# Quantised feed-forward rows: copied into float32r tiles by DMA and transposed in that type, thirteen batches of sixteen

## The chip, the cores and the metric

The kernel runs on one core of one Trainium2 chip. The metric is the device time of that core in microseconds. Before the change the median of 3 runs is 645.22 us (645.11 to 645.31).

## The reference

The input `x` has 16 batches of 256 rows and 256 columns. One layer is computed:

```python
x = x + attn(cond(x))                   # cond: 16-head attention, RMS norm, shift and gain from `cond_256`
                                        # attn: a time mix with a decaying scan, three projections, one out
x = x + ffn(rotate(x))                  # rotate: a quaternion rotation of the columns
# ffn: every matmul has both operands rounded to FP4 in blocks of 16 and scaled back
h = silu(xq @ w_gate.T) * (xq @ w_up.T) # 256 -> 704
y = fp4(h) @ fp4(w_down).T              # 704 -> 256
```

The rounding `fp4` takes the largest magnitude of each block of 16, divides it by 6 to get a scale, rounds each element to the grid 0, 0.5, 1, 1.5, 2, 3, 4, 6, and multiplies the scale back. The change concerns the rows of `fp4(h)`.

## The kernel before

**Stages.** Each batch passes a chain of generators: `ask` (load, query, key and value projections), `attend` (scores, exponentials, weighted values), `leave` (output projection, norm), `mix` (time mix), `rotate`, `hidden` twice, `turn_h` twice, `down`. `hidden(b, tt)` handles 128 of the 256 rows: for each of two column ranges (0 to 384, 384 to 704) PE makes the gate and the up product (L1003), ACT takes a tanh (L1015), DVE forms h in PSUM (L1017, L1019) and `quant_bank` rounds it: DVE instructions on L554 to L557, an absolute value on ACT (L559), two more on DVE (L561, L562), and a product on POOL (L564) that writes the rounded range into an SBUF tile `hq` of 128 x 704 float32, of which there are four buffers.

**Transposing.** `turn_h(b, tt)` makes two calls of `turn_part` (L604 to L609), each of three PE transposes of 128 columns (the last of six has 64) from `hq` into a PSUM bank; ACT copies them into `hT` (L1033 to L1037). The first call reads only the first column range, the second only the second. `down` then multiplies `hT` by `downT` (L1072 and L1079, or L1052 for the late batches). The same `turn_part` serves `out_weights` for the down weights. The last three batches (`late`) use another layout in `rotate` and `down`.

**The order of the work.** There is no scheduler at build time. `ORDER` is a list of 1884 steps written out: `h4` means "run the generator of `hidden(4, 0)` to its next yield". The instructions of PE, ACT, DVE, POOL and SP (SyncE, which issues nearly all DMAs) stand on each engine in just that order, and each engine works through its own list in order, waiting on semaphores. `BANKS` gives, one digit per use, the PSUM bank that each intermediate takes. The letters are a `ask`, t `attend`, l `leave`, m `mix`, r `rotate`, h and i `hidden` for the two row tiles, d and e `turn_h` for them, f `down`; the digit after it is the batch in hexadecimal.

**SyncE's queue.** It issues the input rows (`load_x`, L165), for each spread of queries or keys a store of the split tile to a scratch tensor `kept` in device memory (L704) and eight loads back from it (L708) that wait for the store to land, and the output rows (L1091, or L1064 for late batches).

**float32r.** From batch 2 on the attention scores (L771) take float32r operands: `spread` DMAs float32 bits into a tile declared float32r with a `bitcast`. The plain matmuls and all transposes are float32.

Of the kernel before, what the change touches and what calls it, by code (L numbers as in the profile page):

```python
# [8 lines left out]
F32 = mybir.dt.float32  # L9
BF16 = mybir.dt.bfloat16  # L10
F32R = mybir.dt.float32r
# [7 lines left out]
P = 128  # L19
# [6 lines left out]


ORDER = """
L af L Q L W1 a0 Q L Q a0 Q V0 a0 a1 a0 a0 a1 L W1 a0 W5 Q V0 L Q W1 a1 a1 a1 t0 a1 t0 K t0 W1 K W4 a0 t1 L W5 L
t1 a2 L t1 a2 W5 K W1 t0 W4 K W0 W4 K t0 R V0 a2 a3 M K A a3 a0 t0 L a1 W4 W5 a1 a2 M t0 K A t1 R t1 L t0 t0 t1  # L30
t0 W2 R O t0 t1 t0 W5 M T O W2 t1 t0 t0 a2 t1 V0 t0 a4 t1 L t1 t1 t0 t1 W3 t0 M t0 a2 W4 t1 W1 a2 t1 R V0 A l0
a2 R l0 a2 M W0 l0 V0 W0 W3 l0 W5 M A t1 W3 A t1 l0 W2 t1 T a3 R l0 l0 a2 m0 l0 a3 l1 A l1 W0 m0 m0 R W1 m0 m0
m0 m0 m0 a2 l1 a2 m0 l1 t2 W5 V0 R t2 t2 t2 a3 m0 V1 m0 m0 t2 t2 m0 W3 l1 t2 W3 m0 l1 m0 t2 t2 t2 t2 R t2 t2 t2
R m0 V0 t2 W0 W0 l1 m1 a3 W4 a3 a3 m0 V0 W3 l1 t2 m1 W3 a3 t2 t2 W2 W2 W0 A m1 m1 l2 A m1 m1 W4 l2 r0 m1 l2 m1
l2 r0 a4 a3 m1 m1 l2 l2 m1 m1 l2 m2 m1 m1 l2 m1 a3 m2 t3 a3 t3 m2 t3 t3 t3 m1 a4 t3 r0 r0 t3 r0 t3 a4 t3 t3 t3
m2 a4 t3 t3 a5 m2 W2 a4 V1 m2 t3 a4 t3 r0 t3 m2 m1 r0 t3 r0 a4 r1 m2 m2 a4 r1 t3 r1 r0 a4 W2 a5 a4 l3 l3 a6 m2
l3 V1 r1 m2 r0 a5 i0 a5 m2 i0 r1 r1 m2 i0 l3 V1 a4 t4 r1 m2 t4 t4 h0 i0 V1 t4 t4 i0 V1 m2 a5 t4 i0 h0 i0 h0 h0
t4 t4 i0 V1 t4 t4 t4 t4 i0 t4 a5 l3 t4 a5 r1 l3 r1 t4 m2 m2 h0 l3 a5 m3 l3 m3 t4 V1 a5 m3 i0 i0 a5 r2 r1 t4 h0
t4 m3 m3 r2 i0 m3 h0 a5 m3 l4 l4 a6 m3 l4 m3 m3 i0 a6 a5 l4 m3 m3 V1 a6 m3 t5 m3 t5 i1 i0 m3 t5 t5 i0 m3 t5 t5
e0 h0 i1 i1 e0 a6 t5 i1 t5 t5 t5 t5 h0 t5 t5 m3 i1 l4 t5 r2 a6 r2 t5 r2 l4 a7 t5 l4 i1 i1 d0 h0 i1 a6 h0 m4 r3  # L40
l4 m4 m4 h0 a6 a6 t5 d0 h1 m4 h0 r3 r2 i1 t5 h1 h1 a6 a6 i1 h1 m4 m4 h0 a7 r2 h1 i0 i1 h0 a6 h1 m4 a7 m4 a7 i1
m4 t6 h1 e0 t6 m4 m4 e0 t6 m4 l5 t6 i1 l5 t6 t6 r2 h0 d0 l5 m4 i1 h1 i1 t6 r2 m4 a7 m4 t6 d0 t6 l5 l5 t6 t6 r3
t6 t6 r3 t6 l5 a7 r2 e1 l5 r3 m4 a7 t6 d1 r3 i2 a7 r3 a7 f0 i1 i2 h2 i2 r3 i2 r3 f0 m5 l5 h2 e1 m4 a7 m5 a8 i2
h2 m5 h2 a7 i2 i2 h2 h1 r4 h2 h1 a7 h2 h1 d1 f0 h1 t7 i2 f0 t6 t7 f0 r4 t7 t7 h1 e1 t7 h1 m5 t7 t6 e1 t7 m5 h1
a8 t6 t7 m5 t7 t7 t7 a8 r4 h1 m5 t7 h2 d1 a8 r4 t7 d1 m5 r4 a8 a8 d2 l6 t7 m5 l6 l6 l6 i2 m5 i2 i2 r4 r3 m5 a8
i2 m5 r4 a8 l6 m5 h2 t7 a8 m5 h2 i2 h2 a8 m5 f1 l6 i2 m5 i2 i3 a9 a8 h2 h2 l6 i3 f0 f1 i3 h2 f1 i3 a8 l6 h2 m6
h2 d2 m6 m6 t8 f1 t8 t8 t7 t8 e2 i2 f1 i3 m5 t8 d2 r5 i3 i3 d2 r5 t7 a9 t7 t8 t8 t8 e2 t8 i3 e2 t8 a9 t8 a9 t8
t8 e3 m6 l7 m6 t8 l7 m6 t8 a9 r4 h3 h3 l7 l7 a9 r4 m6 m6 a9 l7 h3 e2 m6 a9 h3 l7 h3 a9 m6 m6 h3 f2 l7 i3 a9 i3
m6 i3 m6 h3 f2 i3 l7 m7 h3 m6 i3 i3 m6 m6 a9 aa m7 h3 i3 h3 h3 f1 h3 f2 m7 a9 e3 t9 t8 t9 t9 t9 f2 m6 r4 d3 f2
i3 t9 r6 h3 h3 t9 d3 e3 t8 h3 r6 t8 t9 h3 aa t9 t9 d3 e3 r5 r5 t9 r5 aa i4 i4 t9 l8 d3 t9 i4 m7 i4 aa i4 ab r5  # L50
h4 l8 i4 r5 m7 l8 h4 i4 f2 l8 aa t9 h4 h4 aa t9 m7 r5 h4 h4 l8 l8 i4 m7 h4 l8 t9 m7 m7 aa aa h4 m7 m7 i4 m7 m7
d4 m8 i4 i4 f3 aa aa l8 m7 m8 h4 m7 i4 i4 f3 m7 h4 m7 i4 m8 aa d4 r7 f3 h4 aa h4 i4 h4 ta f3 ta ta t9 f3 ta r7
ab h4 ac h4 ta e4 r7 t9 ab r7 e4 ta ab i4 ta r7 h4 r5 t9 ta ta r7 m8 ta ta ta ta r7 d4 r5 r6 ab r6 ta m8 m8 e4
m8 ab ab ta r6 m8 m8 m8 m8 l9 ab r6 h5 l9 m8 i5 h5 r6 i5 d4 m8 ab h5 l9 i5 h5 ab i5 e4 h5 i5 h5 h5 h5 ab l9 i5
m8 m8 r6 h5 h5 h5 tb h5 tb ta tb i5 tb m8 m8 r6 ab h5 l9 f4 tb l9 tb tb h5 i5 h5 tb e5 f4 ta ta e5 tb h5 tb tb
tb l9 f4 d5 r8 f4 f4 l9 tb r8 d5 r6 d5 ac m9 f4 tb r7 r8 r7 la tb la h6 h6 la r8 r8 h6 i5 i5 h6 m9 la d5 h6 la
i5 r7 i5 m9 m9 la ac m9 r8 m9 i5 m9 m9 ac i5 m9 la m9 ma m9 ac i6 m9 i7 m9 ac r8 h6 r8 ac m9 i5 i5 m9 i6 i6 ac
e5 m9 ac i7 h6 ac la i7 h6 ma e5 i6 f5 i7 f5 i6 i7 ma i6 i7 m9 f5 ad i6 f5 d6 h7 r9 h6 i6 i7 h6 h6 h6 ac f5 h7
h7 ac d6 tc tc r9 h6 tb h6 h7 tc ad tc ad ae h7 tc tc h6 tb h7 tc ad h7 tc tc tb r9 tc ad tc tc i7 ma h7 tc r9
h6 d6 ad i6 r9 ma tc e6 ma ad tc i6 i6 ma i6 h7 r9 r9 i7 f5 ma i6 r8 ma ad e6 r8 i6 lb ad h7 i7 h7 i6 h8 ma i6  # L60
i7 ma ad i7 ma e6 ma h7 h8 d6 i7 lb ad r9 e6 i7 h8 ma h7 ma r9 lb h7 i7 h8 td lb tc h7 ad td h8 td td td ma h8
lb h8 td e7 lb lb f6 lb f6 e7 mb td f6 i7 mb tc mb h8 ma tc h7 td td d7 f6 ra d7 i8 td f6 td i8 td ra r9 td e7
ae i8 i8 td d7 ra i8 mb i8 e7 f6 ra i8 i9 ae d7 i9 mb ra mb i9 i9 lc ra mb ae mb td h8 mb lc ae h8 i9 lc i8 i9
lc ra ae i9 lc mb h8 ae lc h8 mb h9 lc ra h8 mc ae h8 h9 h9 ra ae mb h9 ae h8 mb mb td d8 lc i8 h9 i8 mb h9 mc
mb f7 ra f7 h8 i8 mb i8 h9 f7 td d8 mc f7 te i8 f7 te rb rb ae te te td e8 i8 rb te te mc h9 i8 mc mc ae rb e8
af f3 rb ld ld rb i9 mc mc mc te ld rb mc te ld te mc mc te te ld mc te i8 te mc mc te mc te d8 af te e8 ld af
te e9 ld md h9 i9 h9 ld h9 te md md md af i9 af d8 mc af i9 md h9 md C rb i9 rb h9 af ha af md i9 e8 i9 md md h9
ha ha md ha f8 md ia ia ha af ia md md ia ha af h9 ia f8 md md i9 f8 ia ia af tf e9 rb tf f8 rc tf tf ia d9 tf
f8 ha tf ia md tf rc tf d9 tf rc i9 ha ia ia tf ia tf tf rc tf tf ia ea e9 e9 ib da rc tf h9 tf d9 ib ib f7 ia
ia le rc rc ib tf f8 le hb ib d9 hb rc tf hb ib le ha le hb le ha ib f9 rc le f9 md le hb ha hb da me ia ha le  # L70
hb ib ha f9 f9 ha ea ha rc ea me ea f9 eb me me me rd ha ib da hb ib me ib me db rd ib rd me rd lf me ib hb da
lf hb ib lf rd rd lf hb lf ib me rd me rd hb lf me hb me lf lf me rd rd ib fa fa hb me db mf eb hb eb hb fa me
db mf mf hc ic hc hc db me fa hc mf re ic fa ic hc ic re hc hc eb re mf ic re ic mf hc re re mf f9 fb re dc hc
fb hc re ic hc dc mf hc mf mf hc re mf mf hc ic ec hc fb mf ic ec ic hc hd ic mf dc mf re id ic ie mf hd ic dc
mf id fb id ic ic id ic hd rf hd id ec ec fc fb id ie rf rf ie id id fb rf fc hd rf ed id hd ed id id hd fc id
hd rf hd rf dd hd id rf ie dd hd he rf id hd he rf id id hd he ed hd he if ie ed hd hd ie if ie ie ie ie ie ie
dd dd he if if ie he he he fa fd ee he fd fd de ee if he ie he if he hf ie fd ie hf he if de he hf if ee he if
ee if ef if hf he hf de de hf fe if fe hf hf hf if hf hf if hf df hf if if fe ef hf hf C fc fe ff df ef ef hf fd
df df C fc fe C ff fc ff ff ff ff ff
"""  # L80


BANKS = """
0123456702 1345670521 3470521364 7320516473 0275164237 5164023571 6043175415 3752406175 2406137541 6035741604
3165042763 1504276315 0246701245 6012465307 2164375023 4756234571 0254371254 3172130671 2507136254 7163204617
3246172530 2615304527 0615627045 6207341502 6731502617 0341635042 3570143527 6013756021 3750425405 6130253607
4163075165 3210746251 0736251063 2416521425 7045273645 0273165407 3416523071 4530276135 2074630146 5370462715
3064537106 2536713460 2153470134 6702346753 6154321675 3421673245 7054763473 1052674273 1520731207 3561403256
1743256412 3054167401 5274301574 3065120373 4561207356 3074305126 4732065704 3215431275 0312670435 1274531604
7531045261 0675105402 5137205146 7250136247 5013473506 2435264053 7415602417 2516427460 3561207314 5017264210  # L90
7640327125 3020425264 6026516106 4106452410 156014205
"""


@with_exitstack
def kernel(
    ctx: ExitStack,
    tc: tile.TileContext,
    x: bass.AP,
    cond: bass.AP,  # L100
    mask: bass.AP,
    w_q: bass.AP,
# [22 lines left out]
    nc = tc.nc  # L125
# [29 lines left out]
    def ps():  # L155
        return bank("ps")
# [41 lines left out]
    early = const.tile([P, T2], F32, tag="early", name="early")  # L198
    nc.scalar.activation(early, mhalf, AF.Exp)
    ident = const.tile([P, P], F32, tag="ident", name="ident")  # L200
    make_identity(nc, ident)


    blank = const.tile([P, P], F32, tag="blank", name="blank")
# [398 lines left out]

    def turn_part(src, k0):  # L604
        pt = ps()
        for k in range(k0, k0 + 3):
            n = min(P, FF - k * P)
            nc.tensor.transpose(pt[0:n, (k - k0) * P : (k - k0 + 1) * P], src[:, k * P : k * P + n], ident)  # L608
        return pt[:, 0 : 3 * P].rearrange("p (k t) -> p k t", t=P)  # L609

    def out_weights(t):
# [407 lines left out]
            nc.vector.scalar_tensor_tensor(h[:, 0:n], th, 0.5, h[:, 0:n], ALU.mult, ALU.mult)  # L1019
            if f0 == 0:  # L1020
                hq = wk.tile([P, FF], F32, tag="hq", name="hq", bufs=4)
                hqs[b, tt] = hq
            yield from quant_bank(h, n, hq[:, f0 : f0 + n])


    def turn_h(b, tt):
        hq = hqs.pop((b, tt))
# [234 lines left out]
```

## Time and profile before

| | |
|---|---|
| median of runs | 645.22 us |
| profiled execution | 645.53 us |
| its span | 643.7 us |
| PE busy | 635.6 us (99%), 3936 matmuls |
| DVE busy | 579.0 us (90%) |
| ACT busy | 391.2 us (61%) |
| POOL busy | 161.4 us (25%) |
| L608, PE transposes of `hq` | 204, durations 272 to 331 ns |
| L564, POOL's product into `hq` | 64, 0.79 us mean |
| DMA traffic | 57.72 MB, 29.4% of 16 engines on SyncE's queue |
| granted PE clock | 1.00 |

The profile is of one execution. A PE instruction's duration runs from its start to a modelled end and overlaps the next; the time from one start to the next is what it costs in a full stream. A plain float32 matmul stands as two records (a weight load and a matmul, twice), a transpose or a float32r matmul as one. In a group's line stand the number of instructions, their busy time, the mean duration of one in ns, and the engine's idle time ahead of them with what ended it. In a line of the timeline stand the start in us, the duration of the merged stretch, and the group.

### The profile page before, as it was taken

To read this page: it belongs to the slowest core of one execution; us is meant where nothing else is said; L and a number is where in the kernel's file an instruction comes from. 1 tells how busy PE (TensorE), PEld (TensorE's weight loads), DVE (VectorE), ACT (ScalarE), POOL (GpSimd) and SP (SyncE) were. 2 spreads that over 40 slices of the span, in tenths; PEclk is the share of its full clock that TensorE was granted. 3 is DMA by queue.
4 is the path that set the end of the run, shared out by engine and by line. 5 is a ranking of instruction groups with operands and counts; after the bars stand their busy time and mean duration, and the time that the engine had idled before them with its cause. 6 is when DMAs were issued, how large, how long until landed. Compare 5 with 4: busy or idle time off the path is not lost.

```text
span 643.7 us, 11304 instructions
## 1 busy us (share of the span) xinstructions
PE 635.6 (99%) x3936; PEld 475.9 (74%) x3936; DVE 579.0 (90%) x1178; ACT 391.2 (61%) x903; POOL 161.4 (25%) x214
## 2 busy tenths in 40 slices
PE   9999999999999999999999999999999999999996
PEld 7568877677777778777777777777877778776675
DVE  7897899889898877999998999999999999999994
ACT  3879784776757577674766546666483755433332
POOL 3353213222231122131221313113130122112220
PEclk9999999999999999999999999999999999999999
DMA  6643525334251425333420334203204100001001
GB/s 169 172 149 120 167 87 174 99 99 133 82 166 35 154 57 166 78 100 116 148 67 18 126 102 149 67 17 131 82 34 151 47 2 16 1 1 35 0 26 46
DMA packets 62848, 57.72 MB, mean 90 GB/s; under 512 B 36912, under 2 KB 40896, under 8 KB 62784
## 3 DMA queue, kind: packets, MB, share of 16 engines
q1 hardware_dynamic: 62416, 56.65, 29.4%
q8 instruction: 33, 0.54, 0.4%
q10 hardware_dynamic: 368, 0.28, 0.1%
q14 instruction: 31, 0.25, 0.1%
HBM read 38.03 MB, written 18.87 MB: 88 GB/s over the span
## 4 chain that ended last, share of the span: by engine, by line
PE 83%; DVE 12%; issue 2%; ACT 1%; DVEq 0%; ACTq 0%
PE ps L632 24%; PE ps L1003 18%; PE ps L793 9%; PE ps L644 8%; PE ps L1072 7%; PE pss L771 5%; PE ps L608 3%; PE ps L965 2%; PE pss L763 2%; DVE v L562 1%; DVE ps L554 1%; PE ps L656 1%; DVE ps L561 1%; DVE ps L1019 1%; PE ps L1079 1%
## 5 line engine op out<-in xcount | busy, mean ns | idle before, releaser
L1003 PE MATMUL ps<-guT,xqT 128*128 128x320 f32 (+1 forms) x512 | 165.6, 461 | 0.6 <-DVE v L562 0.6
L781 ACT ACTIVATE w<-pss 128x512 f32<-128x512 f32 x256 | 133.6, 609 | 32.7 <-PE pss L771 28.8
L1003 PEld LDWEIGHTS ps<-guT,xqT 128*128 128x128 f32 x512 | 94.7, 190 | 42.0 <-DVE v L562 1.7
L564 POOL TENSOR_TENSOR hq<-v,am 128x320 f32<-128x320 f32 (+1 forms) x64 | 50.0, 787 | 175.8 <-DVE v L562 154.4
L698 POOL TENSOR_TENSOR two<-two 128x512 f32<-128x512 f32 x28 | 35.7, 1275 | 114.2 <-ACT two L691 79.1
L793 PE MATMUL ps<-w,v_one 128*32 128x256 f32 x1024 | 63.1, 382 | 0.1
L559 ACT ACTIVATE m<-ps 128x384 bf16<-128x384 f32 (+1 forms) x64 | 29.8, 467 | 53.2 <-DVE ps L557 52.9
L1072 PE MATMUL ps<-hT,downT 128*128 128x256 f32 x260 | 59.6, 379 | 0.0
L1072 PEld LDWEIGHTS ps<-hT,downT 128*128 128x128 f32 x260 | 48.8, 190 | 8.1 <-ACT w L781 0.3
L936 DVE RECIPROCAL den<-den 128x512 f32<-128x512 f32 x16 | 53.5, 3343 | 0.1
L793 PEld LDWEIGHTS ps<-w,v_one 128*32 128x32 f32 x1024 | 31.8, 109 | 25.3 <-ACT w L781 3.6
L1015 ACT ACTIVATE th<-ps 128x320 f32<-128x320 f32 (+1 forms) x64 | 29.8, 469 | 26.9 <-PE ps L1003 26.1
L771 PEld LDWEIGHTS pss<-qT,kT 64*128 64x128 f32 x448 | 31.0, 185 | 19.3 <-issue 8.9
L771 PE MATMUL pss<-qT,kT 64*128 64x256 f32 x448 | 42.6, 306 | 0.1
L561 DVE SCALAR_TENSOR_TENSOR ps<-m,ps 128x384 f32<-128x384 bf16 (+1 forms) x64 | 33.2, 518 | 6.0 <-ACT m L559 5.8
L562 DVE SCALAR_TENSOR_TENSOR v<-m,ps 128x384 f32<-128x384 bf16 (+1 forms) x64 | 33.3, 521 | 4.9
L557 DVE SCALAR_TENSOR_TENSOR ps<-ps,rs 128x320 f32<-128x320 f32 (+1 forms) x64 | 34.1, 533 | 2.2
L554 DVE TENSOR_REDUCE ps<-ps 128x20 f32<-128x320 f32 (+1 forms) x64 | 34.1, 532 | 2.2
L608 PE MATMUL ps<-ident,hq 128*128 128x128 f32 (+1 forms) x204 | 34.5, 283 | 0.4 <-POOL hq L564 0.2
L1019 DVE SCALAR_TENSOR_TENSOR ps<-th,ps 128x320 f32<-128x320 f32 (+1 forms) x64 | 33.2, 518 | 1.1 <-PE ps L1003 0.4
L1017 DVE SCALAR_TENSOR_TENSOR th<-th,ps 128x320 f32<-128x320 f32 (+1 forms) x64 | 32.1, 507 | 0.4 <-ACT th L1015 0.3
L608 PEld LDWEIGHTS ps<-ident,hq 128*128 128x128 f32 (+1 forms) x204 | 22.0, 136 | 13.1 <-issue 4.0
(200 smaller groups left out, 1288.2 us busy)
## 6 DMA issues: line engine op xcount, KB each, us to landing
kept<-two SPq DMA_DIRECT2D x28, 512.0 KB, 3.2
qT<-kept SPq DMA_DIRECT2D x112, 128.0 KB, 2.9
kT<-kept SPq DMA_DIRECT2D x112, 128.0 KB, 2.8
x_sb<-in_x_dram SPq DMA_DIRECT2D x64, 64.0 KB, 2.3
out_dram<-o_sb SPq DMA_DIRECT2D x52, 64.0 KB, 1.9
out_dram<-o_sb SPq DMA_DIRECT2D x6, 128.0 KB, 2.3
raw<-in_L_ffn_w_down_dram SPq DMA_DIRECT2D x2, 352.0 KB, 3.9
raw<-in_L_ffn_w_gate_dram SPq DMA_DIRECT2D x5, 128.0 KB, 3.3
```

The source lines that it names most:

```text
L554: nc.vector.tensor_reduce(top, blk(x), AX.X, ALU.max, apply_absolute_value=True)
L562: nc.vector.scalar_tensor_tensor(v, m, BASE, x, ALU.max, ALU.subtract)
L564: nc.gpsimd.tensor_tensor(blk(dst), blk(v), bc(am), ALU.mult)
L608: nc.tensor.transpose(pt[0:n, (k - k0) * P : (k - k0 + 1) * P], src[:, k * P : k * P + n], ident)
L632: nc.tensor.matmul(pool_tile[:, ot * n : (ot + 1) * n], w[:, ct, ot * P : (ot + 1) * P], src[ct], start=(ct == 0), stop=(ct == E2 - 1),)
L644: nc.tensor.matmul(pool_tile[:, tt * E : (tt + 1) * E], srcT[:, ct, tt * P : (tt + 1) * P], w[:, ct, :], start=(ct == 0), stop=(ct == E2 - 1),
L771: nc.tensor.matmul(quad[2 * s + r][:, i * S : (i + 1) * S], kT[rows_, 2 * r + i, g, ks], qT[rows_, 2 * r + i, g, :], start=True, stop=True,)
L781: nc.scalar.activation(w[kt][:, r].rearrange("p i q -> p (i q)"), quad[r], AF.Exp)
L793: nc.tensor.matmul(pu[32 * r : 32 * r + 32, i * S : (i + 1) * S], vo[:, kt, 8 * g + 2 * r + i, :], w[kt][:, r, i, :], start=(kt == 0), sto ...
L936: nc.vector.reciprocal(flat(den), flat(den))
L1003: nc.tensor.matmul(p_[:, 0:n], xqT[:, ct, tt * P : (tt + 1) * P], guT[:, ct, base : base + n], start=(ct == 0), stop=(ct == E2 - 1),)
L1072: nc.tensor.matmul(pdn[:, 0:S], downT[:, k, h * P : (h + 1) * P], hT[:, k, :], start=(k == 0), stop=False)
```

## The change

For the thirteen batches that are not late, `hidden` issues a DMA on SyncE's queue after each of its two column ranges, from `hq` into a new tile `hr` of type float32r with two buffers. `turn_h` gets `hr` instead of `hq`. `turn_part` sees the type and transposes with an identity of type float32r, `ident_r`, made once by an ACT copy, into a float32r view of the PSUM bank. The bits are moved as they are. `hidden` has two steps more per row tile, 52 in all, so `ORDER` has 1936 steps; it and `BANKS` are written anew throughout. The work of the stages is otherwise the same.

```diff
+    ident_r = const.tile([P, P], F32R, tag="ident_r", name="ident_r")
+    nc.scalar.copy(ident_r, ident)
...
     def turn_part(src, k0):
         pt = ps()
+        fast_ = src.dtype == F32R
         for k in range(k0, k0 + 3):
             n = min(P, FF - k * P)
-            nc.tensor.transpose(pt[0:n, (k - k0) * P : (k - k0 + 1) * P], src[:, k * P : k * P + n], ident)
+            dst = pt[0:n, (k - k0) * P : (k - k0 + 1) * P]
+            nc.tensor.transpose(
+                dst.bitcast(F32R) if fast_ else dst, src[:, k * P : k * P + n], ident_r if fast_ else ident
+            )
...
             if f0 == 0:
                 hq = wk.tile([P, FF], F32, tag="hq", name="hq", bufs=4)
-                hqs[b, tt] = hq
+                if not late(b):
+                    hr = wk.tile([P, FF], F32R, tag="hr", name="hr", bufs=2)
+                hqs[b, tt] = hq if late(b) else hr
             yield from quant_bank(h, n, hq[:, f0 : f0 + n])
-
+            if not late(b):
+                nc.sync.dma_start(out=hr[:, f0 : f0 + n].bitcast(F32), in_=hq[:, f0 : f0 + n])
+                yield
```

A stretch of `ORDER` from the same part of the pipeline, before and after (the whole list is different in this way):

```diff
-m2 a4 t3 t3 a5 m2 W2 a4 V1 m2 t3 a4 t3 r0 t3 m2 m1 r0 t3 r0 a4 r1 m2 m2 a4 r1 t3 r1 r0 a4 W2 a5 a4 l3 l3 a6 m2
+a4 t3 m2 a4 t3 m1 r0 V1 t3 r0 t3 t3 m2 a4 r1 t3 a4 m2 r0 t3 t3 r0 a4 V1 V1 r0 r1 a4 m2 a4 r0 m2 i0 r1 t3 a5 i0
```

## The prediction

> **What bounds the kernel now.** I read the page's first two parts, then the busy time of each engine in stretches of 40 us, the groups of PE instructions with shapes kept apart, PE's timeline around 312 us, and the waits on SyncE's queue. The first part and the slices:
>
> ```profile
> PE 635.6 (99%) x3936; PEld 475.9 (74%) x3936; DVE 579.0 (90%) x1178; ACT 391.2 (61%) x903; POOL 161.4 (25%) x214
> ...
> PE   9999999999999999999999999999999999999996
> ...
> DVE  7897899889898877999998999999999999999994
> ```
>
> PE has no free slice. Its ends are modelled, so I checked starts: over the whole span PE's matmuls begin only some 9.5 us later in sum than their own cadence would let them, 2.5 us of that in the first 6 us and 3.4 us after 560 us. PE really is full. But look at DVE after the first third:
>
> ```profile
> 280.00:320.00 40.00, 39.96 (x257) 31.05 (x256) 36.94 (x74) 25.03 (x51) 10.63 (x11) 1.00 0.40 125
> ...
> 400.00:440.00 40.00, 40.00 (x247) 30.20 (x246) 38.01 (x79) 26.28 (x67) 8.80 (x12) 1.00 0.20 62
> 480.00:520.00 40.00, 40.00 (x242) 29.36 (x241) 38.38 (x81) 20.12 (x47) 7.42 (x8) 1.00 0.31 93
> ```
>
> (Columns: stretch, PE, PE weight loads, DVE, ACT, POOL busy, granted clock, DMA share, GB/s.) DVE is busy 38.0 to 38.4 of 40 us from 360 to 600 us, and the rest are its gaps of a few tens of ns between instructions, 1.3 to 1.9 us per stretch. Its real idle time, 31 us over the span, lies nearly all before 360 us. So in the first half PE alone sets the pace, in the second PE and DVE both. A microsecond taken from PE is worth a microsecond only if the order lets DVE start its work that much earlier.
>
> **The change, part by part.**
>
> *The transposes.* Of 204 transposes on L608, 156 (13 batches, 2 row tiles, 6 each) change to float32r.
>
> ```profile
> 313.21 0.55 PE L608 MATMUL ps<-ident,hq 128*128 128x128 f32 x3
> 313.59 1.03 PE L965 MATMUL ps<-x1T,rotP 128*128 128x256 f32 x4
> 314.46 0.49 PE L608 MATMUL ps<-ident,hq 128*128 128x128 f32 x3
> 314.79 1.89 PE L632 MATMUL ps<-xT,wt_k 128*128 128x256 f32 x8
> ```
>
> Three take 0.33 us from start to next start (314.46 to 314.79), 109 ns each; a group behind a tiled matmul shows 0.38. The price in float32r is not in the trace. Bounds: 109 ns (no gain) and 54 ns (half). The nearest row is the attention score, the only float32r matmul here:
>
> ```profile
> L771 PE MATMUL pss<-qT,kT 64*128 64x256 f32 x448 | 42.6, 306 | 0.1
> L608 PE MATMUL ps<-ident,hq 128*128 128x128 f32 x170 | 31.1, 285 | 0.4 <-POOL hq L564 0.2
> ```
>
> Scores run in pairs on two halves of the rows, and inside a group of eight a pair starts every 118 ns: 256 columns in 118 ns, and two weight loads of 128 columns in the same 118. An f32 matmul of 256 columns takes 216 ns per record, and two records each (L632 shows 128 records for 64 calls). So one float32r pass moves a column in about half the time that an f32 record does, and one float32r weight load costs about 59 ns when it overlaps a matmul. A transpose has one load and 128 columns: I take 60 ns, saving 49.
>
> Two rules of the Trainium skill speak against that. "TensorE: Matmul & The Clock Gate", Back-to-back issue gap, says that a stream of load and matmul pairs at 128 columns sustains one per about 81 ns, not the 56 of an isolated matmul. Then the saving is 28 x 156 = 4.4 us instead of 49 x 156 = 7.7. The same page, Part 4: PE-mode transpose, puts a transpose in a kernel at about 275 ns, most of it access latency, which a type could not change. The trace has both: durations of 272 to 331 ns, but starts 109 ns apart, so the latency is overlapped and the cadence counts. I stay with 60, as the load cadence of 59 is this chip's row, and keep 81 and 109 for the range. PE's sum: -7.7 us (-4.4, 0).
>
> *The copies.* 52 new copies on SyncE's queue, hq to hr, 192 or 160 KB, 9.4 MB beside today's 57.7. Near rows: out rows of 128 KB land in 2.3 us, raw weights of 128 KB in 2.4 to 3.3, a 512 KB store in 3.2; issue takes about 0.45 us. I take 3 us from issue to landing (2 to 5 in a crowd). A half row now needs, after DVE's last quantising instruction (L562), POOL's product (0.79 us), the issue and the landing: about 4.2 us instead of 1. Does the order leave room? Counting the work of PE or of DVE (the larger) that stands in the order between that DVE instruction and the first transpose that reads its half: the old order leaves 1.3 us at the least, the new one at least 5.3 us for all 52 halves. So copies are hidden with 1 us over at the tightest, at no cost to PE; if that cover fails, each late one costs what it is late, and behind the transpose in PE's queue stands everything else. The three late batches keep the short path.
>
> *SyncE's queue.* A copy waits for POOL, and also for the transposes of the row tile two before (hr has two buffers). What stands behind it: attention's stores and loads, x loads, output stores.
>
> ```profile
> SPq L704 <- POOL two L698: 118.5, 21, 22.9
> SPq L1091 <- DVE o_sb L1086: 100.5, 4, 52.0
> SPq L708 <- DMA kept<-two: 73.2, 28, 4.3
> ```
>
> The queue already spends most of its time waiting for others, 52 x 0.45 = 23 us of issue fit in it. The other way: a spread holds the queue for its store's landing (73.2/28 = 2.6 us) and eight loads of 0.59 us, 7.3 us together, and 13 of the 52 copies stand directly behind such loads. I cost this at 0 when the order is kept, and at the third rival when not.
>
> *Small things.* One ACT copy of ident at the start, under ACT's 14 us of idle there: nothing. DVE, ACT and POOL do the same work as before; evictions of hT are unchanged. hq comes free at the copy's landing, not at the transpose.
>
> *The order.* PE's list now has the same instructions in another sequence, so I compared where PE hands over to DVE. Summing PE's start-to-start times up to a place in the order and DVE's work behind that place (durations times 0.93, since they overlap: 650 us of them fill 605 us of busy time and gaps), the largest such sum is about what the time cannot fall below. Before: 531.5 + 110.9 = 642.4 us, against a span of 643.7, so this floor is tight. After, each changed transpose 49 ns cheaper: 523.5 + 113.4 = 636.9. The floor falls by 5.5 us, not 7.7: the rest goes to DVE, which in the new order gets busy earlier (up to 300 us PE and DVE advance side by side) but still ends as the bound. If transposes stay at 109 ns the same sum is 641.2.
>
> The sum: profiled execution 645.5 us (span 643.7), minus 5.5 = 640.0; the median of the runs is 645.2, 0.3 less, so 639.7. I give nothing extra for stalls or for better packing: **639.7 us**.
>
> **The rivals.**
>
> *A, forecast:* PE is relieved and DVE lets 4.4 x 0.7 to 7.7 us of it through: 637 to 642.5. For: no added work on a full engine, and room of 5.3 us before every changed transpose. Against: second half of the span is DVE's too.
>
> *B, the change does not do what it says:* float32r transposes are bound by the weight load, or by both reads together, and stay at 109 ns. Order alone gives 641.2 - 642.4 = -1.2, and some wait for a copy gives +1 to +2: 644 to 646.5. For: a transpose loads new weights each time, and L608's loads are 140 ns long. Against: those loads start 109 ns apart while overlapping matmuls, and the scores' loads at 59.
>
> *C, slower:* copies land after PE wants them, because SyncE's queue serves in order. Place: ten of the 52 copies have less than 8 us in the order between DVE's last instruction and the transpose (5.3 to 7.3). A copy that comes behind a spread waits on average half of its hold, 3.6 us, and in the crowd may land in 5 us instead of 3, so 4.2 us becomes up to 9.8 and the ten miss by 2.5 to 4.5 us. The gain of 5.5 us is cancelled from a mean miss of 0.55 us over the ten; at 1.5 us each, on an engine with no free slice, it is 15 - 5.5: 655, and about 650 where every third falls on a PE that DVE holds up anyway. For: the queue's waits reach 23 and 52 us, and each tile's copy also waits for hr. Against: seven of the ten stand behind 500 us, where attention's traffic has ended (the DMA digits are 0 to 4), and the middle copy has 18 us.
>
> *D:* the second half is DVE's so fully that PE's relief turns into PE idle time: 643.5 to 645.
>
> **How the numbers follow.** A 0.62, B 0.08, C 0.25, D 0.05. A difference of 0.2% (1.3 us) is about what a measurement of this kernel tells from none. A is faster; half of D and a quarter of B are faster; within 0.2% are the other half of D and most of B; C is slower, save a small part that ends level. Faster 0.66, same 0.08, slower 0.26. A's own range is 636 to 642.5. For 8 in 10 I reach below to 635 (all 7.7 us and 2 of waits gone) and above into C to 650.
>
> **What the profile of after would show.** Transposes of hr in threes at about 0.18 us from start to next start (0.24 by the skill's 81 ns, 0.33 if B). PE's busy sum smaller by 5 to 8 us with DVE at 91%. Copies hr from hq landing in 2 to 4 us. In PE's and its loader's waits, hr named by a DMA for less than 2 us in sum; 5 us or more is C. DVE's waits before 360 us smaller by some 5 us; if they stay at 31 us, it is D. What would make the forecast wrong altogether: an order whose waits come from somewhere that neither PE's nor DVE's sums show, such as ACT's evictions of hT standing behind exponentials.

## The result and the profile after

The changed kernel takes 652.07 us, the median of 4 runs (651.33 to 654.54), beside 645.26 (645.11 to 645.35) for the kernel before in the same session: a ratio of 1.0113, with a 95% interval of 1.0086 to 1.0139. It is slower, where faster was forecast, and 2 us above the range. One run of the kernel e9 below (670.68 us, at a granted clock of 0.947) fell in a slower state of the core and is left out of its figures. The profiled execution took 652.05 us with a span of 650.3, 6.5 more than the 643.7 before.

The first two parts of the page of the kernel after:

```profile
PE 633.0 (97%) x3936; PEld 472.6 (73%) x3936; DVE 580.3 (89%) x1178; ACT 393.4 (61%) x904; POOL 161.9 (25%) x214
...
PE   8999999999999999999999999999999999997996
DVE  6988998798998998889998999999899899999993
PEclk9999999999999999999999999999999999999999
```

PE's busy sum fell by 2.6 us only, and PE is no longer full: the slices at the start and at about 595 us show it. The granted clock is full up to 647 us, behind PE's last matmul, so in this execution no part of the loss is a slower array. The same in stretches of 40 us (columns as in the prediction), first before, then after:

```profile
440.00:480.00 40.00, 39.87 (x277) 29.98 (x277) 38.15 (x72) 24.70 (x55) 9.47 (x12) 1.00 0.24 73
560.00:600.00 40.00, 39.62 (x178) 28.73 (x177) 38.06 (x80) 13.35 (x32) 8.20 (x9) 1.00 0.06 14
```

```profile
440.00:480.00 40.00, 38.74 (x217) 29.86 (x216) 36.97 (x72) 25.33 (x61) 9.68 (x13) 1.00 0.34 104
480.00:520.00 40.00, 38.98 (x252) 28.45 (x254) 36.52 (x73) 22.52 (x55) 6.92 (x7) 1.00 0.35 109
560.00:600.00 40.00, 36.62 (x162) 26.48 (x161) 37.91 (x80) 13.30 (x35) 6.57 (x8) 1.00 0.11 32
```

Behind 440 us PE loses 1.1, 1.0 and 3.0 us against before, and DVE, which the forecast wanted busier, loses 1.2 and 1.9 in the first two of them. PE's waits over the span of after, longest first (us in sum, times, longest):

```profile
PE ps L614 <- DMA hr<-hq: 2.3, 2, 1.9
PE pss L779 <- DVE res L1097: 1.3, 1, 1.3
PE ps L614 <- ACT m L563: 1.2, 1, 1.2
PE ps L599 <- DVE num L934: 1.1, 1, 1.1
```

Before, the longest of PE's waits was 1.0 us. The first line names two late copies. The 1.2 and 1.3 us name ACT and DVE; the experiments below show that a DMA stands behind both.

Six transposes before, then six after, each with the matmul behind it, from PE's timeline (start, duration of the merged stretch). Both groups stand behind eight attention scores:

```profile
231.39 0.88 PE L608 MATMUL ps<-ident,hq 128*128 128x128 f32 x6
232.10 1.89 PE L632 MATMUL ps<-yT,wt_ao 128*128 128x256 f32 x8
```

```profile
305.08 0.74 PE L779 MATMUL pss<-qT,kT 64*128 64x256 f32 x8
305.75 0.70 PE L614 MATMUL ps<-ident_r,hr 128*128 128x128 f32 x6
306.29 1.10 PE L973 MATMUL ps<-x1T,rotP 128*128 128x256 f32 x4
```

Six take 0.71 us to the next start before. After, they take 0.54, but the matmul behind them is then held. Counted over all groups, the weight loads inside a group start 84 to 85 ns apart (109 before), and the first full float32 matmul behind the group runs 280 ns to its successor instead of 216. A group of three between full float32 matmuls of 256 columns costs 250 ns instead of 330, so 27 ns each; taken over all 52 groups with their neighbours it is 3.2 us, 21 ns for each of 156.

The copies themselves (KB each, median us from issue to landing):

```profile
hr<-hq SPq DMA_DIRECT2D x26, 192.0 KB, 2.4
hr<-hq SPq DMA_DIRECT2D x26, 160.0 KB, 2.1
```

The trace tells the landing of seven of the 52: six took 2.1 to 2.8 us and one 4.2.

The end of the span is 6.5 us later: PE's last matmul starts 5.3 us later (643.8 for 638.5) and what follows it takes 1.2 us more.

### The profile page after: what moved, and what is told of

Same layout as the page of the kernel before. It is cut to its first block, busy times and chain, and to the rows that moved or that the text cites. A ratio compares the mean times of both kernels' runs of the same rounds, so it can differ in the third digit from the quotient of the medians.

```text
span 650.3 us, 11454 instructions
## 1 busy us (share of the span) xinstructions
PE 633.0 (97%) x3936; PEld 472.6 (73%) x3936; DVE 580.3 (89%) x1178; ACT 393.4 (61%) x904; POOL 161.9 (25%) x214
## 4 chain that ended last, share of the span: by engine, by line
PE 67%; DVE 22%; issue 3%; ACT 3%; DMA 2%; SPq 2%; POOL 0%; DVEq 0%; ACTq 0%; POOLq 0%
PE ps L640 20%; PE ps L1011 14%; PE ps L801 9%; PE ps L652 7%; PE pss L779 5%; PE ps L1084 4%; PE ps L614 2%; DVE v L566 2%; PE ps L973 2%; DVE ps L558 2%; DVE ps L1027 2%; DVE ps L561 2%; DVE ps L565 1%; DVE th L1025 1%; DVE rs L560 1%
## 5 line engine op out<-in xcount | busy, mean ns | idle before, releaser
L563 ACT ACTIVATE m<-ps 128x320 bf16<-128x320 f32 (+1 forms) x64 | 29.7, 464 | 44.3 <-DVE ps L561 44.0
L566 DVE SCALAR_TENSOR_TENSOR v<-m,ps 128x320 f32<-128x320 bf16 (+1 forms) x64 | 33.3, 521 | 4.7
L1025 DVE SCALAR_TENSOR_TENSOR th<-th,ps 128x320 f32<-128x320 f32 (+1 forms) x64 | 32.1, 506 | 4.3 <-ACT th L1023 4.1
L947 POOL TENSOR_TENSOR yT<-num,den 128x512 f32<-128x512 f32 x16 | 20.5, 1278 | 58.4 <-DVE den L944 50.9
L565 DVE SCALAR_TENSOR_TENSOR ps<-m,ps 128x320 f32<-128x320 bf16 (+1 forms) x64 | 33.1, 518 | 1.1 <-ACT m L563 0.9
L652 PE MATMUL ps<-wt_v,xT 128*128 128x256 f32 x128 | 30.7, 382 | 0.0
```

Of the source, the lines that this page charges most:

```text
L566: nc.vector.scalar_tensor_tensor(v, m, BASE, x, ALU.max, ALU.subtract)
L652: nc.tensor.matmul(pool_tile[:, tt * E : (tt + 1) * E], srcT[:, ct, tt * P : (tt + 1) * P], w[:, ct, :], start=(ct == 0), stop=(ct == E2 - 1),
```

## The experiments

Three things changed at once: the order with its banks, the type of the transposes, the copies. The first four runs take them apart. Theory after the result: the order and late copies both cost more than the transposes give. Rivals: the order alone; the copies alone; the float32r transposes bring nothing. Diffs of `ORDER` and `BANKS` are given in words.

**e1, the order alone.** The new `ORDER` with its `BANKS`, no copies, float32 transposes. `hq` gets six buffers instead of four and two of `hr`; the yields stay, so that the steps count as in after.

```diff
-                hq = wk.tile([P, FF], F32, tag="hq", name="hq", bufs=4)
-                if not late(b):
-                    hr = wk.tile([P, FF], F32R, tag="hr", name="hr", bufs=2)
-                hqs[b, tt] = hq if late(b) else hr
+                hq = wk.tile([P, FF], F32, tag="hq", name="hq", bufs=6)
+                hqs[b, tt] = hq
...
             if not late(b):
-                nc.sync.dma_start(out=hr[:, f0 : f0 + n].bitcast(F32), in_=hq[:, f0 : f0 + n])
                 yield
```

> The new order with neither copies nor float32r: rows stay in hq (6 buffers, the room that hr had), 156 transposes in plain float32. If the new order itself loses the time (theory 1: its start and its last 60 us leave PE waiting whatever the type), this stays at 652 or goes up by the 3 us that float32 transposes cost more: 652 to 656. If late copies lose it (theory 2), taking them away gives back about 5 us of waits and pays 3 us for the type: 648 to 650. If neither, and only the small gain of the type was mis-sized, it is near the old kernel: 645 to 647.

Measured: 652.63 us, 1.0099 (1.0082 to 1.0116). The order alone costs 6.4 us, nearly the whole loss of after. Its span is 7.1 us longer than before. PE's late starts (beyond the time to the next start that the same pair of instructions usually shows) sum to 16.1 us instead of 11.5: 3.0 more in the first 80 us, 2.7 more between 560 and 600, 1.1 less elsewhere. (By the profile's own idle gaps of 150 ns and more it is 7.7 us instead of 2.5.) What follows PE's last start grew by 1.7, and 0.8 lies in the cadence of the other sequence and was not placed. The stretch around 595 us of e1, in windows and on the timeline (in brackets the idle time ahead and what ended it):

```profile
560.00:600.00 40.00, 37.16 (x162) 26.68 (x161) 37.77 (x79) 13.19 (x35) 6.31 (x7) 1.00 0.06 14
```

```profile
593.59 1.34 PE L1011 MATMUL ps<-guT,xqT 128*128 128x320 f32 x4 [0.89 <-DVE v L566]
595.15 0.52 PE L614 MATMUL ps<-ident,hq 128*128 128x128 f32 x3 [0.21 <-DVE th L1025]
596.59 0.52 PE L614 MATMUL ps<-ident,hq 128*128 128x128 f32 x3 [0.93 <-issue]
597.67 2.64 PE L1081 MATMUL ps<-hT,downT 128*128 128x256 f32 x11 [0.56 <-DVE th L1025]
```

PE stands four times in 4 us: the two `hidden` row tiles, their transposes and `down` follow each other in PE's list. What they wait for is a PSUM bank (one of the eight that take PE's products), not data. The lines name L566 and L1025, on which DVE reads the bank of h, or of the gate product, for the last time. Walking `ORDER` and `BANKS` with the trace's times bears this out: each of the four begins 0.05 to 0.15 us after the last reader of its bank has ended (the third one's is an ACT copy on L978), while the two transposes' rows were written 0.7 and 1.2 us before; and when each wait began, none of the eight banks was free, so no other digit would have helped there. Over the whole span 4.1 of e1's 7.7 us of idle time end this way, beside 0.8 of 2.5 us before. No copy and no float32r is in this kernel.

**e2, copies without the type.** After, with `hr` declared float32.

```diff
-                    hr = wk.tile([P, FF], F32R, tag="hr", name="hr", bufs=2)
+                    hr = wk.tile([P, FF], F32, tag="hr", name="hr", bufs=2)
```

> The new order with the 52 copies, but hr is plain float32 and all transposes are float32: the type alone undone. The profile of the changed kernel shows a group of three at about 250 ns in place of 330 between full matmuls, about 330 in place of 386 behind tiled ones: 3 us over 52 groups. Type worth its 3 us: 654 to 656. Type worth the 7.7 us that was forecast: 659. Type worth nothing, because PE waits elsewhere anyway: 651 to 653.

Measured: 657.61 us, 1.0157 (1.0119 to 1.0196), with a wide spread (653.36 to 658.86). Against e1 the copies cost 0.58%, 3.7 us. In the profiled execution (658.86 us) most of this is the clock. PE waits 1.74 us for keys up to 507 us and 1.90 us for a copy up to 603 us, and behind each wait the granted clock is 0.50 for 3.41 us:

```profile
504.85:508.26 3.41, 1.67 (x14) 1.21 (x15) 3.34 (x8) 0.89 (x3) 1.64 (x2) 1.00 0.45 150
508.26:511.67 3.41, 3.41 (x11) 2.31 (x10) 1.52 (x4) 1.76 (x5) 0.00 (x0) 0.50 0.00 0
600.42:603.83 3.41, 1.51 (x10) 1.23 (x11) 3.20 (x9) 1.88 (x5) 0.18 (x1) 1.00 0.42 112
603.83:607.25 3.42, 3.42 (x10) 2.70 (x9) 3.17 (x8) 0.92 (x3) 0.84 (x1) 0.50 0.09 20
```

At half the clock 3.41 us are 1.7 us of PE's work lost, 3.4 us for both. e1's trace has no such stretch before its end.

**e3, the type without copies, in the new order.** As e1, but POOL writes its product into a float32r tile. POOL then rounds the value to float32r, where the copy moves the bits; nothing else is left out here or in the later kernels of this kind.

```diff
+                hq = wk.tile([P, FF], F32 if late(b) else F32R, tag="hq", name="hq", bufs=6)
```

> The new order, float32r transposes, no copies: POOL's product writes the row as float32r at once, which rounds the quantised values (that part of the computation is changed). Against the changed kernel only the copies are gone. Theory 2 (late copies): 645 to 648. Theory 1 (order): 650 to 652.

Measured: 648.69 us, 1.0051 (1.0032 to 1.0071). Against e1 the type brings 0.48%, 3.1 us; after, which has the copies too, is 0.62% or 4.0 us slower than e3. So the sum is 6.4 for the order, minus 3.1 for the type, plus 4.0 for the copies: 7.3 us, where 1.13% of 645.26 is 7.3. (The intervals of e3 and after don't touch; each term is uncertain by about 1 to 2 us, and the sum closes by its making.)

PE's list in e3 is the same as in after, so each late copy can be found by laying one against the other. From 20 to 330 us there is no difference. Then there are three places: at 335 us PE starts 1.25 us later, at 459 us 1.7, at 500 us 0.3. The first two on the timeline of after:

```profile
336.22 0.42 PE L614 MATMUL ps<-ident_r,hr 128*128 128x128 f32 x3 [1.23 <-ACT m L563]
...
461.80 0.71 PE L779 MATMUL pss<-qT,kT 64*128 64x256 f32 x7 [1.26 <-DVE res L1097]
...
597.51 0.40 PE L614 MATMUL ps<-ident_r,hr 128*128 128x128 f32 x3 [1.90 <-DMA hr<-hq]
```

and SyncE's queue before them, first in after, then in e3:

```profile
328.58 3.79 SPq L1035 DMA_DIRECT2D hr<-hq  x2
...
447.41 0.53 SPq L1035 DMA_DIRECT2D hr<-hq  x1
449.35 0.39 SPq L712 DMA_DIRECT2D kept<-two  x1
454.33 5.01 SPq L716 DMA_DIRECT2D kT<-kept  x8
```

```profile
448.55 0.39 SPq L712 DMA_DIRECT2D kept<-two  x1
451.46 5.12 SPq L716 DMA_DIRECT2D kT<-kept  x8
```

At 335 us the second of two copies was issued at 331.86, as soon as POOL's product ended, and landed at 336.08, 4.2 us later; the transposes start at 336.22. The ACT instruction that the line names can't be the cause: in e3 the same transposes start 1.2 us before that instruction ends. The DMA view of 331.8 to 336.3 us, in 40 slices:

```profile
GB/s 0 0 0 0 0 0 0 0 0 0 146 273 396 259 355 312 194 168 148 80 0 0 0 0 0 14 14 0 14 14 14 14 27 80 168 166 155 73 134 157
...
q8 instruction: 1, 0.02, 2.2%
...
hr<-hq SPq DMA_DIRECT2D x1, 192.0 KB, 4.2
```

The trace's packets tell what the tail of 14 GB/s is. Of the copy's 128 rows 120 had been moved by 333.73 us; the last eight went one after another from 334.63 to 335.57. A single packet of 16 KB, of the queue that the profile calls `instruction`, took from 333.03 to 334.64. Eight rows are a sixteenth of the copy, and there are 16 DMA engines, so the copy's last rows seem to have queued behind that packet on one engine. (A packet's record does not name its engine; this is read from the times.) Two other kernels repeat it: in e2 the packet took 1.65 us and the same copy landed in 4.23, in e15 0.95 us and 3.47.

At 459 us it is no copy that is late. The store of the keys was issued at 449.35, behind a copy, 0.8 us later than in e3. Of its 256 packets 240 had begun by 451.67; the last 16 began at 452.18, when another `instruction` packet (451.27 to 452.19) had ended. So its loads began 5.0 us after the store instead of 2.9, and the scores of the next batch waited for the keys. In e3 that packet came at 451.11, when the store's last packet had begun. The copy cost another transfer, and the traffic of the `instruction` queue, 33 packets in before as in after, made both late.

That these two are the copies' doing is seen in the other kernels: e2 and e15 (below), which have the copies, wait at both places too (1.22 and 1.39 us, 0.55 and 0.52), and e1 and e3, which have none, at neither. In e15 the profile names them rightly, as `DMA hr<-hq` and `DMA kT<-kept`.

The third line, 1.90 us, is a late copy too (issued at 595.32, landed in 2.2), but e3 has 0.93 us and then another 0.68 at the same place without any copy, so the copy takes the place of waits there.

PE's last start is 2.7 us later than in e3, which is these places less 0.4 us at the start. The other 1.6 us of the two spans' difference lie behind PE's last start: 0.2 at the issue of the last store and 1.4 from there to the end of the span. That last stretch takes 3.9 us before, 3.4 in e3, 4.7 in e1 and 4.8 in after, with and without copies, and stays unexplained.

**e4, the type without copies, in the old order.** The kernel before, with the tile of POOL's product declared float32r in thirteen batches, and the new `ident_r` and `turn_part`. One line decides:

```diff
-                hq = wk.tile([P, FF], F32, tag="hq", name="hq", bufs=4)
+                hq = wk.tile([P, FF], F32 if late(b) else F32R, tag="hq", name="hq", bufs=4)
```

> The old order and only the type changed: POOL's product writes the row as float32r (rounded, which changes that part of the computation), 156 transposes in float32r. PE's saving by the profile of the changed kernel is about 3 us; the old order keeps DVE and PE together. If the type's gain passes through: 641.5 to 643. If DVE holds the second half in the old order: 643.5 to 645. By the forecast of 7.7 us on PE: 637.5 to 640.

Measured: 643.62 us, 0.9964 (0.9953 to 0.9976). It is faster than both kernels (and, as in e3, its values are rounded, which the copy's are not). The page and the six transposes at 231 us of e4:

```profile
PE 633.5 (99%) x3936; PEld 473.6 (74%) x3936; DVE 578.3 (90%) x1178; ACT 391.0 (61%) x904; POOL 161.4 (25%) x214
```

```profile
231.39 0.69 PE L612 MATMUL ps<-ident_r,hq 128*128 128x128 f32 x6
232.00 1.97 PE L638 MATMUL ps<-yT,wt_ao 128*128 128x256 f32 x8
```

0.61 us instead of 0.71, at the same place of the same sequence. The type brings 2.3 us of the 3.2 that the starts give.

**e5, e6, e7, where the order loses: a first try.** The first 300 steps of one order and the rest of the other, both ways, and the old order for 1650 steps (to 552 us) with the new end; each kernel's banks dealt anew, to the bank that has been free longest.

```diff
-ORDER = new
+ORDER = the first n steps of one order + the steps that are left, as the other has them
-BANKS = new
+BANKS = at each use the bank that came free first
```

> No copies, no float32r. The order alone is split: the old order for its first 300 steps (97 us in the old trace), then the steps that are left in the new order's sequence, with PSUM banks dealt out anew. PE's late starts in the new order alone are 6.7 us in the first 80 us against 3.7 in the old. If the start is one of the new order's two losses: 3 us back, 649 to 650. If the loss is all in its last 90 us: 652 to 653. If it is spread over the whole list: 651 to 652.

> The mirror of it: the new order's first 300 steps, then what is left in the old sequence; float32, no copies. If start and end losses stand apart and add up: old kernel plus 3 us, 648.5 to 649.5. If the start's waits are made good later, since DVE has idle time before 360 us: 645.5 to 647.

> The old order to its step 1650 (552 us in the old trace), then the new sequence of what is left; float32, no copies. In the new order alone PE starts 2.7 us later between 560 and 600 us than in the old, and the span ends 7.0 us after PE's last start instead of 5.2. If the last steps' own sequence is at fault: 649 to 651. If the end is only where an earlier lag of DVE shows (what was done by 552 us decides): 645.5 to 647.

Measured: 1.0315 (1.0283 to 1.0346), 1.0214 (1.0184 to 1.0244), 1.0345 (1.0313 to 1.0377). All are slower than either order, so they say nothing of the order. They say something of the banks: up to 552 us e7 has the very steps of the kernel before, and it is late by 3.2 us at 100 us, 8.7 at 300 and 12.5 at 540. Up to there it differs in the PSUM banks and in having six buffers of `hq` instead of four; e13 (below), with the same six buffers and the old banks, is level with the kernel before (within 0.1 us) for the 111 us that its steps are the same.

**e9, e10, e13, the same with each order's own banks.** Cut where each use can keep its digit: e9 has 340 old steps and then the new order, e10 the new order to step 1450 and then the old one, e13 both (old start, new middle, old end). All in float32 without copies, so to be laid beside e1.

```diff
-BANKS = at each use the bank that came free first
+BANKS = each stretch with the digits of its own order
```

> The split of the order once more, at a place where each part can keep the PSUM banks of its own list (not one digit is changed): 340 old steps (112 us), then the rest in the new sequence; float32, no copies. The earlier split dealt the banks anew, and lost 12 us already inside the stretch where its steps stood as in the old kernel, so it told of banks. If the new order's start is one of two losses: 3 us less than the new order alone, 649 to 650. If the loss is spread or at the end: 651.5 to 653.

> The new order and its banks for 1450 of 1936 steps, then the rest in the old sequence with the old banks (no digit changed); float32, no copies. If the new order's end (2.7 us of PE's late starts between 560 and 600 us, 1.7 us more after PE's last start) is the second loss: 4 us less than the new order alone, 648 to 649. If what was done before decides the end: 651.5 to 653.

> 340 old steps, the new sequence to step 1450, the old sequence to the end, banks as in each list (no digit changed); float32, no copies. If start (1.7 us) and end (4.2 us) are the new order's whole loss: 645 to 646.5, level with the old kernel. If the middle loses too, or the two overlap: 647 to 649.

Measured: e9 650.03 (three runs, 650.01 to 652.76), 1.0072 (1.0054 to 1.0090); e10 647.42, 1.0033 (1.0020 to 1.0046); e13 648.47, 1.0050 (1.0035 to 1.0065). The end is the larger part: with the old end 4.3 of e1's 6.4 us are gone, which is what the trace of e1 gave for its end (2.7 + 1.7). The stretch in e10:

```profile
560.00:600.00 40.00, 39.61 (x179) 29.12 (x178) 37.81 (x78) 14.08 (x34) 8.19 (x9) 1.00 0.06 14
```

PE is full again there. The remaining 2 to 3 us were not settled: by itself the old start brings 1.7 us (the intervals overlap a little), on top of the old end nothing. Part of the reason is the first seam: in the traces of e9 and e14 PE waits there 0.57 and 1.08 us within 2 us, and the granted clock is 0.50 for the next 3.41 us. Start, middle and the two seams are not told apart.

**e14, the type once more.** e13 with `hq` in float32r, as in e3.

> The same order with float32r transposes and no copies (POOL's product writes the row as float32r, rounded). Type worth 2.5 us as in the old order: 2.5 us under e13. Type worth 3.9 us as in the new order, because the new middle lets DVE use PE's time: 641 to 642.5, and then the fastest of all.

Measured: 647.32 us, 1.0024 (1.0015 to 1.0033). The type brings 0.26%, 1.7 us. The clock at the seam blurs this too. e13's runs are 647.5 and 647.8 us at a mean clock of 1.00, 649.2 and 649.9 at 0.997; e14's are two of 645.3 at 0.999 to 1.00 and ten of 647.1 to 648.5 at 0.996 to 0.997. At the full clock the type brings 2.3 us, as in e4. By the ratios it is worth 1.7 to 3.1 us over three orders.

**e12, all sixteen batches in float32r**, in the old order.

```diff
-                hq = wk.tile([P, FF], F32 if late(b) else F32R, tag="hq", name="hq", bufs=4)
+                hq = wk.tile([P, FF], F32R, tag="hq", name="hq", bufs=4)
```

> The old order, no copies, float32r written by POOL's product for all 16 batches (the rounding of the values is changed, as in the run with 13). 36 more transposes, 12 groups, of which each saves 27 to 80 ns: 0.3 to 1 us on PE, but the last three batches stand where DVE has no gap at all. Against the old order with 13 batches (ratio 0.9964): 0.995 to 0.9965.

Measured: 643.88 us, 0.9979 (0.9971 to 0.9987), no better than thirteen.

**e8, the copies on POOL's queue**, so that SyncE's stays as it was.

```diff
-                nc.sync.dma_start(out=hr[:, f0 : f0 + n].bitcast(F32), in_=hq[:, f0 : f0 + n])
+                nc.gpsimd.dma_start(out=hr[:, f0 : f0 + n].bitcast(F32), in_=hq[:, f0 : f0 + n])
```

> The changed kernel as it is, but its 52 copies are issued by POOL after its own product instead of SyncE. The copies cost 3.4 to 4 us in float32r (changed kernel against the run without copies), and the two traces differ at three places: PE waits 1.25 us for hr at 335 us, 1.7 us for keys at 459 us, 1.6 us more at the very end. If SyncE's in-order queue makes these: 648.5 to 650. If it is the landing time itself, whoever issues: 651.5 to 653. If POOL's issue is dear and holds up its products: 655 and more.

Measured: 656.78 us, 1.0155 (1.0122 to 1.0187). The page of e8:

```profile
PE 634.4 (97%) x3936; PEld 473.8 (72%) x3936; DVE 584.0 (89%) x1178; ACT 393.0 (60%) x904; POOL 191.8 (29%) x266
```

POOL is busy with 52 more instructions for 30 us, about 0.57 us a copy, and DVE's busy sum is 3.7 us larger than in after for the same work. So POOL's queue is no cure; by its interval it is not better than SyncE's, and likely worse. (1.7 us of its profiled execution are a stretch of 3.41 us at half the clock, behind a wait of 2.21 us for a copy at 599 us.)

**e15, a third buffer of `hr`.** If copies are late because their tile is still being read, this helps.

```diff
-                    hr = wk.tile([P, FF], F32R, tag="hr", name="hr", bufs=2)
+                    hr = wk.tile([P, FF], F32R, tag="hr", name="hr", bufs=3)
```

> The changed kernel with three buffers of hr instead of two. SyncE waits 19.1 us in 8 waits for transposes to release a buffer, and what stands behind it waits too. If that makes the copies' 3.4 to 4 us: 648.5 to 650. If the copies lose by landing late and by holding back the keys' store: 651 to 652.5, no change.

Measured: 652.40 us, 1.0110 (1.0096 to 1.0125), the same as after. The buffers are not it.

**e11, the copies in the old order.** Half-row tiles in six buffers, which is room for three row tiles, each copy straight behind POOL's product, so that no step is added.

```diff
     def quant_bank(src, n, dst, copy=()):
...
+        if copy:
+            hr = copy[0]()
+            copy[2].append(hr)
+            nc.sync.dma_start(out=hr[:, 0 : copy[1]].bitcast(F32), in_=copy[3])
...
+                copy = (lambda: wk.tile([P, 384], F32R, tag="hr", name="hr", bufs=6), n, halves_, hq[:, f0 : f0 + n])
```

> The old order with copies and float32r transposes: each copy is issued by SyncE straight behind POOL's product, into half-row float32r tiles (6 of them). The old order leaves 1.3 us at the least between DVE's last quantising instruction and the transpose, where product, issue and landing of 2.1 to 2.4 us need about 4. If the copies' latency has no cover there: each short half waits 1 to 3 us, 6 to 10 of them outside the late batches: 650 to 665. If copies are free when the order is good: 643 to 645, like the old order with float32r and no copies.

Measured: 674.13 us, 1.0450 (1.0416 to 1.0483). PE's waits in e11, then a place of its timeline, SyncE's queue before it, and the windows around it (in the windows the granted clock is the third number from the end):

```profile
PE ps L618 <- DMA hr<-hq: 11.2, 8, 2.8
PE pss L783 <- DMA kT<-kept: 5.1, 4, 2.8
PE ps L618 <- DVE th L1029: 4.1, 1, 4.1
```

```profile
377.57 0.58 PE L618 MATMUL ps<-ident_r,hr 128*128 128x128 f32 x3 [4.12 <-DVE th L1029]
```

```profile
369.75 5.05 SPq L720 DMA_DIRECT2D qT<-kept  x8
374.90 0.54 SPq L570 DMA_DIRECT2D hr<-hq  x1
```

```profile
374.00:378.00 4.00, 0.43 (x4) 0.46 (x4) 3.97 (x7) 0.69 (x2) 1.98 (x3) 0.92 0.82 276
378.00:382.00 4.00, 4.00 (x13) 2.63 (x12) 3.20 (x7) 1.28 (x4) 0.82 (x1) 0.65 0.37 105
```

This wait is not DVE's: POOL's product for these transposes ended at 372.54, but SyncE had eight loads of queries to issue first and sent the copy at 374.90, as rival C had it. The old order left 1.3 us for the path that now takes 4, and pays 29 us for it. Four stretches of 3.41 us at half the clock, behind such waits, are 6.8 us of it. So the allowance that the new order makes is needed for the copies, and the new order as such is worth nothing without them. The copies of after with the old end of the order were not tried.

**DVE's idle time as a gauge.** Idle time of DVE behind 360 us, from gaps of 150 ns and more, beside the ratio:

| kernel | idle, us | ratio |
|---|---|---|
| e4, e12 | 1.0, 1.0 | 0.9964, 0.9979 |
| before | 1.4 | 1 |
| e14, e10, e13 | 2.0, 2.5, 2.9 | 1.0024, 1.0033, 1.0050 |
| e3, e9, e1 | 4.4, 5.7, 5.6 | 1.0051, 1.0072, 1.0099 |
| e15, after | 5.4, 6.0 | 1.0110, 1.0113 |
| e8, e2 | 6.2, 10.7 | 1.0155, 1.0157 |
| e5, e7 | 11.4, 11.4 | 1.0315, 1.0345 |
| e11 | 20.7 | 1.0450 |
| e6 | 4.3 | 1.0214 |

Where both engines are full, DVE's idle time there goes roughly with the loss, while PE's busy sum (633.0 after, 633.5 in e4) tells nothing of which kernel is fast. It is a gauge of that part only: e6 loses its time before 360 us, where DVE idles 40.7 us instead of the 29.8 of before.

## Why the prediction was wrong

*"The order" failed, and it is the main step.* It took the largest sum of PE's time up to a place and DVE's behind it for what the time would follow: 642.4 before, 641.2 for the new order with slow transposes. e1 is just that kernel, and its span is 650.8, 9.6 us above the sum. A sum of work up to a place contains no wait for a PSUM bank, such as those in the chain of `hidden`, transposes and `down` at 595 us, no other wait at the start, and nothing of what stands behind PE's last matmul. Nor was the sum as tight before as it looked (1.3 us below the span). In the trace of before DVE's durations add up to 624 us, not 650, and 605 of 624 is 0.97, not 0.93. Redone so, the largest sum is near 639 us before and near 640 in e1 (an estimate from the two traces). It tells the two orders apart by 1 us, where the runs do by 6.4.

*"The transposes": right in kind, less than half in size.* 49 ns each became 21; 7.7 us became 3.2 by the starts. The step took the load cadence of the scores, 59 ns, where a pair of loads goes to two halves of the rows in 118. A transpose's load goes to all rows and shows 84 to 85 ns, and the matmul behind the group pays another 65. The rule that was weighed and not taken, 81 ns for a load and matmul pair in the Trainium skill ("TensorE: Matmul & The Clock Gate", Back-to-back issue gap), agrees with the trace. The 275 ns of the same page's Part 4 are near the durations here (284 ns mean before, 265 after), and don't set the cost. Put into the floor by its share, 21 ns would have given 639.4 instead of 636.9.

*"The copies … at no cost to PE" failed; with the next step it is 4 us.* The usual landing was right (2.1 and 2.4 us, forecast 3), and PE waited for hardly any of the 52. But the room was smaller than counted: 5.3 us at the least by sums of work, while at 335 us DVE's last instruction ended at 330.9 and PE was ready for the transposes at 335.0. In these 4.1 us POOL's product, the issue and a landing of 2.4 us would have fitted; the landing of 4.2, behind an `instruction` packet, did not. The forecast's 2 to 5 us "in a crowd" had the size, its sum the middle.

*"SyncE's queue", costed at 0, failed with it.* The step asked only whether the copies come in time; the store of keys behind one of them went out 0.8 us later, into another `instruction` packet, and PE waited 1.3 us for its loads. That is rival C's queue, with copies and loads in each other's way, at one or two places instead of ten and at 4 us instead of 15; the packets that made them late were in no rival. Seven of C's ten places stand behind 500 us, and there the queue was indeed free.

*What held:* PE and DVE both bound behind 360 us; small things cost nothing that the trace shows; the waits named for a copy came to 2.3 us, just above the 2 that the forecast allowed, though the 1.2 us at 335 us stand under another name. "DVE's waits before 360 us smaller by some 5 us" did not come: that idle time is 29.4 us after and 29.8 before. PE's busy sum fell by 2.6 us, where 5 to 8 was forecast. The measured time is nearest to C's 650 to 655, but that is luck: by e1 most of the loss is the order itself, which no rival had as its cause. Two slips change nothing: A's lower end is 637 in one place and 636 in another, and DVE's busy time from 520 to 560 us is 37.9, not 38.0 or more.

## What to carry to other kernels

A floor of work tells what an order can't beat, not what it takes; before a change that also reorders a tight schedule is believed, run the new order alone, and look which PSUM bank each wait stands for. Price a new transfer by what it delays on its queue as well as by its own landing, and that landing by its slow cases (4.2 us here) where the room is short, and price a group of transposes by the start of the second matmul behind it. Here one type in one tile declaration, written (and rounded) by the engine that makes the data, was worth 0.36%, and moving the same data by DMA with an order made for it lost 1.13%.

## What was unexpected of the hardware

A float32r transpose of 128 columns starts with its weight load every 84 to 85 ns (float32: 109), and a float32 matmul behind the group is held for some 65 ns. The choice of PSUM bank, at the same order of steps, cost 12.5 us of 540 (e7). A copy of 192 KB that usually lands in 2.4 us took 4.2 when one packet of the `instruction` queue came in its way.

A PE wait can cost more than itself. In e11 the clock is 0.50 for 3.41 us around the end of the 4.1 us wait (0.65 over the 4 us of the window), which is another 1.6 us or so of PE's work. The Trainium skill ("TensorE: Matmul & The Clock Gate", Part 1) says that after an idle window of about 3.4 us the array runs at half its clock, and this wait fits that. Here less was enough: 1.74 and 1.90 us in e2, 0.57 and 1.08 us close together in e14. In the traces the clock keeps one value for stretches of 3.41 us or a multiple of it. Leaving out the end of a span, each stretch at 0.50 follows one in which PE was idle for 48% or more (51 and 56% in e2: 1.67 and 1.51 us busy of 3.41), and none follows one in which PE was idle for less; between 48 and 53% both are seen. In after, the wait of 1.90 us fell across two stretches, 44 and 42% idle, and the clock stayed at 1.00. So it matters where a wait falls among these stretches, and the runs of one kernel differ in it: e14's fall into two groups, and after's four have mean clocks of 0.998, 0.998, 0.996 and 0.994.
